# Score steps of the first attention unit between fine steps of a feed-forward block's down sums, and one sequence's sum transfers moved within a round

## The chip, the core and the metric

The kernel runs on one core of a Trainium2 chip. The metric is device time in microseconds of one execution. Five engines work side by side, each through its own instruction queue: PE (TensorE, matmuls; PEld is its weight loads), DVE (VectorE), ACT (ScalarE), POOL (GpSimd), and SP, which here only issues transfers. ACT issues some transfers too. The median before the change is 820.93 us of 3 runs (820.42 to 822.25).

## What is computed

Two sequences of 1024 tokens and 256 channels pass through a "macaron" block: half a feed-forward (FFN), causal attention, half the same FFN.

```
x = x + 0.5 * ffn(layernorm(x))
x = x + attention(layernorm(x))          # 32 heads of 8, 8 key/value heads, rotary, causal
x = x + 0.5 * ffn(layernorm(x))

ffn(x):  h = silu(x @ w_gate) * (x @ w_up)          # 256 -> 1024
         keep of every four neighbours of h the two largest by size
         return h @ w_down                          # 1024 -> 256  ("down sums")
attention: softmax(q k^T / sqrt(8), causal) v, then @ Wo + bo
```

## The kernel before

**Blocks.** The 2048 tokens are four blocks of 512 (`tb` 0 to 3; blocks 0 and 1 are the first sequence). For a block the FFN makes gate and up products (`gate_up`, L238, matmuls at L252), the two-of-four mask in three parts (`mask`, L268: comparisons, ranks, and at L292 the masking of h), and the down sums (`down_half`, L303, matmuls at L307). A block's down sums are two halves of 16 matmuls, each half into one PSUM tile; `down_half` is a generator that yields after every two matmuls. A float32 matmul leaves two records in the trace. `add` (L332, L340 on DVE) adds a finished half to x; `add_aside` (L324) does it with ACT (L329) and POOL (L330).

**Order in the first FFN.** PE and DVE follow an order written out by hand, the string of `first.run` (L941): `g` a step of gate and up, `m` a part of a mask, `d` half of a block's down sums (the generator `down`, L296, runs a half through), `a` an add, `l` layernorm, and `p` a step of the attention's generator: projections of the first sequence, and last the preparation of its first unit. The string ends `g3 p m m m d2 d2 a a`: block 2's down sums on PE beside block 3's last mask on DVE, then two adds.

**Attention.** A unit is one key/value head of one sequence with its four query heads; 16 units, 8 for each sequence. `prepare` (L521) transposes a unit's queries and keys on PE (L529), copies them with ACT (`stage`, L537), and spreads them by 16 transfers into the unit's `qT` and `kT` (L550, L557), and by two more of zeros (L543); for the very first unit SP and ACT share the issuing. `pass1` (L568) makes scores (L584, diagonal masks L599) into one of three PSUM buffers (`ps_big`), and DVE takes negated row maxima from it (L613). `negated` gathers them, POOL splits them (L415, L416), `shift` transposes them (L640) and writes them by four transfers into `qT` (`mrow`, L651). `pass2` makes the scores again, turned and shifted (L669), ACT takes exponentials (L679), and `weighted` sums values (L706). A finished half is copied to `oT` and stored to DRAM (`avs`, L717).

**Rounds.** `round_(n)` (L858) goes through one list, `order` (L770): first-pass steps `p1` (18 in a round) of the current unit, second-pass steps `p2` and `av` of the one before, `prep` of the next. In round 0 there is only a first pass. There PE alternates with `beside_first`, which is `down_slowly(3)` (L318), block 3's down sums through one PSUM tile: two fine steps after each of the first, third, fifth and so on up to the twelfth `p1`, and the rest after the list (L889). Ahead of round 0 POOL clears the buffers of the next two units (`rows`, L397 and L400), in memory that the first FFN gave back. In the rounds PE and POOL keep the order of the text; the other engines and the transfer queues are ordered by a planner, by costs of its own.

**Outputs.** When a sequence's eighth unit has finished a half (`av 2` or `av 9`, L818), `output` (L719) starts: its first step reads the stored sums and heads back by eight transfers on SP (L730, L731); its second takes reciprocals on DVE (L733) and sends them around through DRAM (L735, L737). For the first sequence the first step is taken at once (L825), in rounds 8 and 9, and the second later, after `av 5` of rounds 9 and 10 (L881).

Of the kernel before, what the change touches and what calls it, by code (L numbers as in the profile page):

```python
# [35 lines left out]
def macaron_kernel(  # L36
# [23 lines left out]
    ps_tr = ctx.enter_context(tc.tile_pool(name="ps_tr", bufs=1, space=PSUM))  # L60
    ps_acc = ctx.enter_context(tc.tile_pool(name="ps_acc", bufs=1, space=PSUM))
# [161 lines left out]
    class FFN:  # L223
# [79 lines left out]
        def down_half(self, tb, t2, pool, tag):  # L303
# [11 lines left out]
                        yield  # L315
            self.adds.append((tb, t2, o))

        def down_slowly(self, tb):  # L318

            for t2 in range(2):  # L320
                yield from self.down_half(tb, t2, ps_acc, "acc")
                self.add_aside()
# [26 lines left out]
        def run(self, plan, gens, outs=()):  # L349

            make = {"g": self.gate_up, "d": self.down}
            with tc.manual_schedule(engines={mybir.EngineType.PE, mybir.EngineType.DVE}):
                for op in plan.split():
                    if op == "m":
                        if next(self.masks[0], 0) == 0:
                            self.masks.pop(0)
                    elif op == "a":
                        self.add()  # L360
                    elif op == "o":
                        if next(outs[0], 0) == 0:
                            outs.pop(0)
                            next(outs[0])
                    else:
                        if op not in gens:
                            tb = int(op[1])
                            gens[op] = (
                                make[op[0]](tb)
                                if op[0] in make  # L370
                                else layernorm_T(tb, lambda tb=tb: self.normed(tb), halves=tb == 0)
                            )
                        next(gens[op])

# [9 lines left out]
    def attention(actx, beside_first, beside_last, outs):  # L386
# [413 lines left out]
        def parsed(order):  # L800
            return [(op[0], *map(int, op[1:])) for op in map(str.split, order.split(";"))]

        ops = parsed(order)
        PAIRS = [("av", k) for k in (1, 3, 5, 7)]
        first = max(i for i, op in enumerate(ops) if op[0] == "p1" and op[1] < 3)
        units = [(b, g) for b in range(B) for g in range(NKV)]
        made = {}
        beside = []
        divisions = []

        def step(op, prev, cur, nxt):
            kind, *arg = op
            if kind == "p1" and cur is not None:
                cur.pass1(*steps1[arg[0]], arg[1:] or (0, 1))
            elif kind == "p2" and prev is not None:
                es = prev.pass2(*steps2[arg[0]], arg[1:] or (0, 1))
                made.setdefault(arg[0], (prev, {}))[1].update(es)
            elif kind == "av" and arg[0] in made:  # L818
                unit, es = made.pop(arg[0])
                qh, kbs = steps2[arg[0]]  # L820
                last = arg[0] in (2, 9)
                unit.weighted(qh, kbs, es, last)
                if last and unit.g == NKV - 1:
                    outs.append(output(unit.b, qh))
                    next(outs[-1])  # L825
                    if unit.b < B - 1:
                        divisions.append(outs[-1])
            elif kind == "neg1" and prev is not None:
                prev.negated(1)
            elif kind == "shift":  # L830
                unit = prev if arg[0] == 1 else cur
                if unit is not None:
                    unit.shift(arg[0])
            elif kind == "prep" and nxt is not None:
                nxt.prepare()
# [5 lines left out]
        prev, cur = None, Unit(*units[0])  # L841
        cur.prepare()
        yield
        rctx = ExitStack()
        right = rctx.enter_context(tc.tile_pool(name="att2r", bufs=1, side="right"))
        rows(right)
# [7 lines left out]
        def a_step():  # L854
            while beside and next(beside[0], beside) is beside:
                beside.pop(0)

        def round_(n, prev, cur):  # L858
            nxt = Unit(*units[n + 1]) if n + 1 < len(units) else None
            if n == 1:  # L860
                beside.append(second)
            if nxt is not None and nxt.b == 1:
                for _ in second:
                    pass
            firsts = 0
            for i, op in enumerate(ops):
                step(op, prev, cur, nxt)
                if i == first and cur is not None:
                    cur.negated(0)
                if n == 0 and i == first:  # L870

                    nc.scalar.activation(warm, cur.maxima[0][:, 0, 6:7], AF.Exp, scale=0.0)
                if n == 0 and op[0] == "p1":
                    firsts += 1
                    if firsts <= 12:
                        for _ in range(2 * (firsts % 2)):
                            next(beside_first, None)
                if n > 0:
                    for _ in range(2 if op in PAIRS else op[0] in ("av", "prep")):
                        a_step()  # L880
                if n > NKV and op == ("av", 5) and divisions:  # L881
                    next(divisions.pop(0))
            return cur, nxt

        engines = {mybir.EngineType.PE, mybir.EngineType.Pool}
        with tc.tile_pool(name="att_round0", bufs=2, side="right") as late["2"]:
            with tc.manual_schedule(engines=engines):
                prev, cur = round_(0, prev, cur)
                for _ in beside_first:  # L889
                    pass  # L890
# [6 lines left out]
        with tc.manual_schedule(engines=engines):  # L897
            for n in range(1, len(units)):
                prev, cur = round_(n, prev, cur)
        rctx.close()  # L900
        yield
        with tc.manual_schedule(engines=engines | {mybir.EngineType.DVE}):
            for op in parsed(last_order):
                if op[0] == "b":
                    next(beside_last, None)
                else:
                    step(op, prev, None, None)
            for _ in beside_last:
                pass

    with ExitStack() as fctx:
        actx = ExitStack()
        gens, outs = {}, []

        def second_starts():


            while not second:
                yield
            made = [outs.pop(0), outs.pop(0)]  # L920
            lns = [
                layernorm_T(tb, lambda tb=tb: second[0].normed(tb), copy=nc.vector.tensor_copy)
                for tb in range(2)
            ]

            for k in (0, 1):
                next(made[k])
            yield
            for gen in (made[0], made[0], lns[0], made[1], made[1], lns[0], lns[1], lns[0]):
                next(gen)  # L930
                yield
            for gen in (lns[1], lns[1]):
                next(gen)
                yield

        second = []
        with last_units:
            first = FFN(0, False, f0 := ExitStack(), wd_sb, last_pool)
            att = attention(actx, first.down_slowly(NTB - 1), second_starts(), outs)
            with f0:  # L940
                first.run(  # L941
                    """
                    l0 l0 l0 l1 g0 l1 g0 l2 g0 g0 l2 g0 m l1 g0 g0 l2 m g0 m g1 m g1 m g1 m
                    g1 g1 m g1 d0 m a d0 l3 a p g1 p g1 m g2 m p g2 m g2 m p p p g2 p d1 m m
                    g2 m d1 a a l3 g2 p g2 l3 p g2 m p g3 p p m g3 p p m g3 g3 g3 m g3 m g3
                    m g3 p m m m d2 d2 a a
                    """,
                    {"p": att},
                )
            next(att)  # L950
        next(att)
        early_ctx.close()
        second.append(FFN(1, True, fctx))
        for _ in att:
            pass
        second[0].run(
            """
            o g0 g0 g0 g0 m o g0 g0 o m g0 o g0 m g1 m g1 m g1 m g1 o g1 l2 g1 d0 m l2 g1 g1
            m m m l2 a d0 g2 m g2 o g2 g2 o m a g2 m o l3 g2 l3 g2 d1 m m g2 m m l3 d1 g3 m
            g3 g3 g3 a a g3 m g3 m g3 m g3 d2 m m m a d2 d3 a d3 a a  # L960
            """,
            gens,
            outs,
        )
        actx.close()
# [56 lines left out]
```

## Time and profile before

| | us |
|---|---|
| median of 3 runs (lowest, highest) | 820.93 (820.42, 822.25) |
| the profiled execution's own time | 824.67 |
| its span, first to last instruction | 822.9 |
| third block's down sums on PE | 166.42 to 180.45 |
| first score step of the first unit | 180.37 |
| first second-pass score (round 1 opens) | 210.58 |
| distance of unit preparations (L529) in a round with nothing beside it, as 386.74 to 412.34 | 25.6 |

Times in the profile are microseconds from the span's start. A timeline line has start, length, engine (a q behind it is the engine's queue issuing a transfer), line, operation, tiles written and read, shape, count, and in brackets the engine's idle time before it and what ended it. A line of the view by windows has the window, its length, then busy time and number of instructions of PE, PEld, DVE, ACT and POOL, then the granted share of the TensorE clock, the transfer engines' share, and GB/s. The page's row PEclk gives the granted clock in 40 slices, in tenths.

### The profile page before, as it was taken

How to read it: one execution, taken by the hardware profiler on the slowest of the kernel's cores; microseconds unless marked ns; L12 is line 12 of the kernel's file. 1: busy time of each engine (PE TensorE's matmuls, PEld its weight loads, DVE VectorE, ACT ScalarE, POOL GpSimd, SP SyncE). 2: the span in 40 equal slices, each digit the busy share in tenths (PEclk: the TensorE clock that was granted, in tenths of full speed). 3: DMA queues.
4: the chain of work that ended last, by engine and by line, in shares of the span. 5: the costliest groups of instructions: out<-in, count | busy, mean ns of one | idle time of the engine just before them, and what ended most of it. 6: DMA issues, size and time to landing. Idle time of an engine off the chain costs nothing.

```text
span 822.9 us, 13949 instructions
## 1 busy us (share of the span) xinstructions
PE 786.1 (96%) x5344; PEld 426.4 (52%) x5344; DVE 654.7 (80%) x871; ACT 426.9 (52%) x531; POOL 236.2 (29%) x443
## 2 busy tenths in 40 slices
PE   5999999998899999999999999999999999999998
PEld 2447574476544444454444444444445445657466
DVE  4797999898768796888888788888885479788692
ACT  1331313211677776877787687878877423122210
POOL 3000294821265465464222322233223100000000
PEclk9999999999999999999999899999999999999999
DMA  8100000022213222311333323322202200000001
GB/s 276 31 0 2 0 2 0 0 41 41 33 27 64 44 46 50 67 31 44 66 68 70 93 65 68 56 44 51 57 28 92 74 1 16 1 26 1 11 16 51
DMA packets 31010, 36.03 MB, mean 44 GB/s; under 512 B 12896, under 2 KB 20960, under 8 KB 30944
## 3 DMA queue, kind: packets, MB, share of 16 engines
q1 hardware_dynamic: 29118, 31.85, 17.2%
q10 hardware_dynamic: 1826, 3.29, 1.2%
q8 instruction: 42, 0.69, 0.4%
q14 instruction: 24, 0.20, 0.1%
HBM read 10.75 MB, written 10.75 MB: 26 GB/s over the span
## 4 chain that ended last, share of the span: by engine, by line
PE 71%; DVE 22%; ACT 4%; issue 1%; POOL 1%; DMA 0%; DVEq 0%; ACTq 0%
PE gu L252 20%; PE av L706 16%; PE s L584 9%; PE s L669 9%; PE o L307 9%; DVE maxima L613 8%; ACT e L679 3%; DVE h L292 2%; PE pr L474 2%; PE oo L753 2%; DVE h L262 1%; DVE sg L261 1%; DVE b L275 1%; PE s L599 1%; PE hT L529 1%
## 5 line engine op out<-in xcount | busy, mean ns | idle before, releaser
L613 DVE TENSOR_REDUCE maxima<-s 128x2 f32<-128x1024 f32 (+2 forms) x288 | 343.2, 1220 | 67.2 <-PE s L584 44.3
L679 ACT ACTIVATE e<-s 128x1024 f32<-128x1024 f32 x288 | 287.4, 1023 | 83.4 <-PE s L669 75.1
L706 PE MATMUL av<-e,vaug 128*32 128x512 f32 (+3 forms) x1536 | 158.5, 501 | 0.0
L685 POOL TENSOR_SCALAR_AFFINE_SELECT e<-e 128x256 f32<-128x256 f32 (+1 forms) x224 | 98.3, 451 | 201.5 <-ACT e L679 201.0
L584 PE MATMUL s<-kT,qT 64*128 64x512 f32 (+3 forms) x768 | 133.3, 386 | 14.6 <-ACT e L679 11.7
L669 PE MATMUL s<-qT,kT 64*128 64x512 f32 (+3 forms) x768 | 134.7, 395 | 3.1 <-DVE maxima L613 2.2
L252 PE MATMUL gu<-xnT,wg_sb 128*128 128x512 f32 x256 | 122.3, 600 | 0.7 <-ACT xnT L206 0.7
L252 PE MATMUL gu<-xnT,wu_sb 128*128 128x512 f32 x256 | 120.4, 593 | 0.0
L307 PE MATMUL o<-wd_sb,h 128*128 128x256 f32 x512 | 116.6, 386 | 0.9 <-DVE x L340 0.8
L584 PEld LDWEIGHTS s<-kT,qT 64*128 64x128 f32 x768 | 67.9, 187 | 82.7 <-ACT e L679 37.2
L307 PEld LDWEIGHTS o<-wd_sb,h 128*128 128x128 f32 x512 | 98.1, 193 | 18.5 <-issue 3.7
L669 PEld LDWEIGHTS s<-qT,kT 64*128 64x128 f32 x768 | 67.5, 186 | 62.1 <-DVE maxima L613 32.9
L260 ACT ACTIVATE sg<-gu 128x512 f32<-128x512 f32 x64 | 38.0, 593 | 113.6 <-PE gu L252 113.6
L263 ACT ACTIVATE a<-h 128x512 f32<-128x512 f32 x64 | 40.3, 630 | 104.9 <-DVE h L262 104.8
L252 PEld LDWEIGHTS gu<-xnT,wu_sb 128*128 128x128 f32 x256 | 48.9, 191 | 61.8 <-issue 61.8
L261 DVE TENSOR_TENSOR sg<-sg,gu 128x512 f32<-128x512 f32 x64 | 43.6, 681 | 46.1 <-ACT sg L260 46.0
L252 PEld LDWEIGHTS gu<-xnT,wg_sb 128*128 128x128 f32 x256 | 48.6, 192 | 54.6 <-issue 50.0
L181 POOL TENSOR_TENSOR rstd<-ve,neg_half 128x4 f32<-128x4 f32 x12 | 12.2, 1015 | 194.1 <-DVE ve L179 192.3
L706 PEld LDWEIGHTS av<-e,vaug 128*32 128x32 f32 x1536 | 34.1, 109 | 50.2 <-issue 38.8
L262 DVE TENSOR_TENSOR h<-sg,gu 128x512 f32<-128x512 f32 x64 | 43.9, 687 | 2.2
L599 PE MATMUL s<-half_id,half_mask 64*128 64x64 bf16 (+1 forms) x768 | 43.8, 205 | 0.0
L292 DVE SCALAR_TENSOR_TENSOR h<-w,h 128x512 f32<-128x512 bf16 x64 | 43.7, 743 | 0.0
(80 smaller groups left out, 562.4 us busy)
## 6 DMA issues: line engine op xcount, KB each, us to landing
avs<-oT SPq DMA_DIRECT2D x32, 256.0 KB
qT<-stage SPq DMA_DIRECT2D x124, 64.0 KB
kT<-stage SPq DMA_DIRECT2D x124, 32.0 KB
qT<-mrow SPq DMA_DIRECT2D x128, 4.0 KB
heads<-avs SPq DMA_DIRECT2D x16, 128.0 KB
out<-x SPq DMA_DIRECT2D x7, 256.0 KB
wu_sb<-in_wu SPq DMA_DIRECT2D x2, 512.0 KB
wg_sb<-in_wg ACTq DMA_DIRECT2D x2, 512.0 KB
```

Of the source, the lines that this page charges most:

```text
L252: nc.tensor.matmul(out=gu[:, i, :], lhsT=w_sb[:, kc, gb, j, :], rhs=self.xnT[tb][:, kc, :], start=(kc == 0), stop=(kc == 1),)
L261: nc.vector.tensor_tensor(sg, sg, gu[:, 0, :], ALU.mult)
L262: nc.vector.tensor_tensor(h[:, j, :], sg, gu[:, 1, :], ALU.mult)
L292: nc.vector.scalar_tensor_tensor(h[:, j, :], w[:, j, :], at, h[:, j, :], op, ALU.mult)
L307: nc.tensor.matmul(out=o[:, i, :], lhsT=self.hms[tb][k // 4][:, k % 4, bass.ts(2 * t2 + i, P)], rhs=self.wd_sb[:, k // 4, k % 4, :], start ...
L584: nc.tensor.matmul(out=to[:, i, s, bass.ds(col, n)], lhsT=self.qT[strip, pair, bass.ts(qt, P)].bitcast(FR), rhs=self.kT[strip, bass.ds(kc ...
L599: nc.tensor.matmul(out=last.rearrange("p (t n) -> p t n", n=P)[:, :, bass.ts(h, STRIP)], lhsT=half_mask[strip, h, :], rhs=half_id[strip, N ...
L613: ins = nc.vector.tensor_reduce(dst, src, AX.X, ALU.max, negate=True)
L669: nc.tensor.matmul(out=to[:, i, s, bass.ds(col, n)], lhsT=self.kT[strip, bass.ts(kb, P)].bitcast(FR), rhs=self.qT[strip, pair, bass.ds(q0, ...
L679: nc.scalar.activation(e, to, AF.Exp, scale=SCALE)
L685: nc.gpsimd.affine_select(out=first, in_=first, pattern=[[0, 2], [0, len(pairs)], [1, P]], compare_op=ALU.is_ge, fill=0.0, base=0, channel ...
L706: nc.tensor.matmul(out=self.av[32 * i : 32 * i + 32, TB - n : TB], lhsT=vaugs[self.b][:, kb, bass.ds(self.g * VW, 32)], rhs=es[i][:, bass. ...
```

## The change

Block 2's down sums get a finer generator (`down_finely`, letter `e`), and the first six `p1` steps of the first unit move out of round 0 to stand between them: 11 fine steps and the first add, then score and fine step in turn, six times, then the second add. Round 0 skips those six, and takes one fine step of block 3's sums after each of its 12 remaining score steps, and one more after every fourth. The first step of the first sequence's two outputs, with its eight transfers, is kept back until `av 4` of the same round.

```diff
+        def down_finely(self, tb):
+
+            for t2, (pool, tag) in enumerate(((ps_acc, "acc"), (ps_tr, "tr"))):
+                yield from self.down_half(tb, t2, pool, tag)
...
-            make = {"g": self.gate_up, "d": self.down}
+            make = {"g": self.gate_up, "d": self.down, "e": self.down_finely}
...
-                        next(gens[op])
+                        next(gens[op], None)
...
+        HEAD = 6
...
+        stored = []
...
                     outs.append(output(unit.b, qh))
-                    next(outs[-1])
                     if unit.b < B - 1:
-                        divisions.append(outs[-1])
+                        stored.append(outs[-1])
+                    else:
+                        next(outs[-1])
...
         cur.prepare()
         yield
+        scores = [op for op in ops if op[0] == "p1"]
+        for op in scores[:HEAD]:
+            step(op, prev, cur, None)
+            yield
...
             for i, op in enumerate(ops):
+                if n == 0 and op in scores[:HEAD]:
+                    continue
                 step(op, prev, cur, nxt)
...
                     firsts += 1
-                    if firsts <= 12:
-                        for _ in range(2 * (firsts % 2)):
-                            next(beside_first, None)
+                    for _ in range(1 + (firsts % 4 == 0)):
+                        next(beside_first, None)
...
                 if n > NKV and op == ("av", 5) and divisions:
                     next(divisions.pop(0))
+                if op == ("av", 4):
+                    for out_ in stored:
+                        next(out_)
+                    divisions.extend(stored)
+                    stored.clear()
...
-                    m g3 p m m m d2 d2 a a
+                    m g3 p m m m e2 e2 e2 e2 e2 e2 e2 e2 e2 a e2 e2 p e2 p e2 p e2 p e2 p e2 p e2 a
```

## The prediction, made before the change was run

> **What bounds the kernel now.** The first view is the page. It is a TensorE kernel, and the profiled execution has a few stretches of lowered clock.
>
> ```profile
> span 822.9 us, 13949 instructions
> PE 786.1 (96%) x5344; PEld 426.4 (52%) x5344; DVE 654.7 (80%) x871; ACT 426.9 (52%) x531; POOL 236.2 (29%) x443
> PEclk9999999999999999999999899999999999999999
> ```
>
> A busy PE is not yet a PE doing useful work, so the second view is PE's timeline across the edit, from the third block's down sums (L307, 64 records, two to a matmul) to the first second-pass scores (L669), which open round 1.
>
> ```profile
> 166.42 14.03 PE L307 MATMUL o<-wd_sb,h 128*128 128x256 f32 x64
> 180.37 0.51 PE L584 MATMUL s<-kT,qT 64*128 64x256 f32 x4
> 181.85 1.99 PE L307 MATMUL o<-wd_sb,h 128*128 128x256 f32 x8 [0.84 <-DVE x L340]
> ...
> 189.93 0.50 PE L584 MATMUL s<-kT,qT 64*128 64x512 f32 x2
> 190.26 0.23 PE L599 MATMUL s<-half_id,half_mask 64*128 64x64 bf16 x4
> 190.33 0.48 PE L584 MATMUL s<-kT,qT 64*128 64x512 f32 x2
> 190.65 0.23 PE L599 MATMUL s<-half_id,half_mask 64*128 64x64 bf16 x4
> 190.82 1.99 PE L307 MATMUL o<-wd_sb,h 128*128 128x256 f32 x8
> ...
> 200.40 0.50 PE L584 MATMUL s<-kT,qT 64*128 64x512 f32 x2 [0.78 <-DVE maxima L613]
> ...
> 204.51 6.14 PE L307 MATMUL o<-wd_sb,h 128*128 128x256 f32 x16
> 210.58 0.50 PE L669 MATMUL s<-qT,kT 64*128 64x512 f32 x2
> ```
>
> PE works through the third block's sums without a gap. Then 18 score steps alternate with the fourth block's sums, and from about 199.6 PE only follows DVE's maxima. The last 16 records take 6.14 us where 16 x 0.219 = 3.5 us would do (14.03/64 = 0.219). The third view, DVE's timeline, shows why scores could not simply come earlier: DVE is at the last mask (L292) until 181.2, its first maxima start at 182.32, and later it has nothing for 4.15 us.
>
> ```profile
> 178.71 2.49 DVE L292 SCALAR_TENSOR_TENSOR h<-w,h 128x512 f32<-128x512 bf16 x4
> 181.12 1.28 DVE L340 SCALAR_TENSOR_TENSOR x<-o,x 128x512 f32<-128x512 f32 x2
> 211.49 3.73 DVE L613 TENSOR_REDUCE maxima<-s 128x4 f32<-128x1024 f32 x3 [4.15 <-PE s L599]
> ```
>
> The fourth view, busy time by window, explains the slow tail: the granted clock (the column after POOL) is halved for 6.83 us right after a window in which PE was busy 1.43 of 3.41 us, and once more in round 10.
>
> ```profile
> 199.19:202.60 3.41, 1.43 (x8) 0.37 (x4) 3.41 (x4) 0.00 (x0) 0.00 (x0) 1.00 0.14 24
> 202.60:209.43 6.83, 6.68 (x22) 4.90 (x23) 4.74 (x7) 0.00 (x0) 0.00 (x0) 0.50 0.01 2
> 308.41:311.82 3.41, 3.41 (x24) 1.42 (x26) 2.74 (x3) 2.46 (x3) 3.41 (x4) 0.50 0.52 82
> 465.42:472.25 6.83, 6.83 (x51) 3.21 (x49) 4.24 (x5) 3.59 (x4) 1.73 (x4) 0.50 0.32 48
> ```
>
> The last view is what the first unit's scores need: 16 transfers of K and Q. Their last issue is
>
> ```profile
> 176.61 0.54 ACTq L557 DMA_DIRECT2D qT<-stage  x1
> ```
>
> and its last semaphore count stands in the trace at 179.04.
>
> **The stage, part by part.** Everything up to 166.42 stays. I price PE's pieces from the timeline. A diagonal score step takes 0.40 us before another score (189.93 to 190.33) and 0.49 before a down sum (190.33 to 190.82). In the same way a step off the diagonal costs 0.36, a two-tile step 0.55, a step with eight masks 0.60 to 0.65. Eight down records up to the next score last 1.92 (188.00 to 189.92), that is 1.75 of work and 0.17 of change-over, so a step of two matmuls (four records) costs 0.876 + 0.17 = 1.05. Before a transpose (L529, L640) the change-over is missing. These prices put the work from 180.37 at 23.3 us, an end at 203.7. The trace ends at 210.58, so 6.9 us are lost: 0.84 for the add, 2.6 to the clock, some 3.4 to DVE's maxima. That is all the change can win here.
>
> After the change PE does 11 fine steps (44 records, 9.64 us), and is at the first score at 166.42 + 9.64 = 176.06. In the trace of before this score waits for nothing, because 20 records more stand ahead of it. Now it meets the transfers: 179.04 - 176.06 = 3.0 us of new idle time, and in PE's order the other ten matmuls of the block are queued behind it. The issue times do not move (ACT's copy of the stage at 168.90 comes from L529 at 165.45), so I take 3.0; with the last transfer needed only by the second pair the wait is 2 at least.
>
> From 179.05: six score steps 3.00 (0.65, 0.36, 0.55, 0.49, 0.55, 0.40), five fine steps 5.25, the next unit's transposes (`prep`) 0.86: 188.16. The three score buffers do not hold PE: DVE's maxima start at 181.8 after one add (0.64) instead of two, every 1.14 us, and the fourth score comes at 183.8, after the first maxima's end at 183.0. The second add (0.64) now stands behind the sixth maxima, where DVE has slack.
>
> Then round 0: twelve scores 5.20, 16 fine steps of 0.876 = 14.02, eleven change-overs less the saving before the transposes 1.73, the shift's transposes 0.54: 21.49, so 209.65 without waits. Two waits come in. POOL's memsets of the next two units' buffers wait for the last matmul of the third block (before at 180.56, <-PE o L307); that now ends at 187.0. They and the memset of vaug take 6.0 us (180.56 to 186.56), the split of the maxima 0.53 more, so the shift's transposes can start at 193.65 while PE is there at 192.53: 1.12 us. If the vaug memset slips behind the split it is 0.4; I take 1.12, the order the trace shows. And the fourth block's second half follows its first with one score between, while ACT must copy out the first (0.60): 0.4 us. Round 1 then opens at 211.2, 0.6 later than before. SP's transfers for the next unit move 1 to 2 us later, end near 201 and are needed after 211: nothing. The add and the fine steps as instructions are the same ones as before: nothing.
>
> So the idle time and the clock loss are won back (6.9), and paid for by 3.0 + 1.5 of new waits and some 3 us of change-overs (18 alternations where there were 8).
>
> **The clock.** A 3.0 us gap in a dense stretch is itself a low window. The three drops start 105.8 and 157.0 us apart, 31 and 46 times 3.413, so the windows lie on a fixed grid which the work meets anywhere. The Trainium skill ("TensorE: Matmul & The Clock Gate", section "What's actually happening") says that the half clock comes after at least one *idle* window of about 3.4 us, free-running. By that rule a gap of 3.0 never fills a window and costs nothing: 0.6 us in all. The row disagrees: a window busy 1.43 of 3.41, never idle for long, was followed by the half clock. By the row a window needs about 2 us of idle; a 3.0 us gap gives that in about two grid positions of three. I take the row. The price is one window at half speed in work that PE bounds, 3.41/2 = 1.7 us; two windows, as at 202.60, would be 3.4, but there PE had little to do in the first, so 308.41 is the nearer row. The stage: 0.6 + 1.7 = +2.3 us, none without the drop to +4 with two.
>
> **The transfers in mid-round.** Eight transfers for each of two outputs move behind `av 4`; no instruction is added. In the trace the first lot runs at 434.03 to 437.6, behind a zeros transfer, and the mrow transfers at 437.74 are 0.2 late against a clean round of 25.65 us; the second lot splits the four mrow transfers (the fourth goes at 459.57, some 6 us late), yet the scores that need it start at 461.44, as far behind their neighbour (0.70) as in a clean round. So SP's delay is hidden and its removal wins nothing. What rounds 9 and 10 do lose, 1.30 and 2.86 us beyond 25.65 (438.0, 464.9, 493.45), is two reciprocals of 0.94 us on DVE (443.13, 462.86) and the half clock at 465.42. The reciprocals stay, and the planner places them. I take 0; both hidden would be -1.3, both worse +1.3, and the clock there either way 2.9.
>
> **The sum.** 822.9 + 2.3 = 825.2 us of span for an execution like the profiled one (824.67 with what lies around it). That one stands 3.7 above the median of 820.93, with the same stage in it, so I add the difference to the median: 823.3.
>
> **Rivals.**
> Clock kept: the grid or the rule is kind, and the stage alone counts: +0.6, 821.5, or 820.8 with the memset out of the way. For it: PE is dense on both sides of the gap. Against: the row at 199.19.
> Faster: in rounds 9 and 10 the earlier sums let DVE take both reciprocals in idle time, so PE is not held at the next unit's transposes (0.80 at 464.94), no low window forms and no half clock follows: up to -4.2, with half of it likely to be seen in an average execution, -2.1 to -2.9; with the clock kept at the gap as well, 818.7. It decides from 1.3 us saved there on. Against: the emission of the reciprocals is unmoved.
> Not what it says: SP's order is planned, and the transfers moved in the text may be issued where they were; the stage alone remains, inside the first two cases.
> Much slower: two windows at half clock, or the sums at the head of SP's queue holding zeros and mrow for a round: 825.5 and more.
>
> **Chances.** Half clock at the gap, 823.3 (821.8 to 825): 0.42, of it 0.06 within 0.2%. Clock kept: 0.24, all within. Faster: 0.26. Much slower: 0.08. So faster 0.26, within 0.2% (1.6 us, about what a measurement of this kernel can tell) 0.30, slower 0.44. The range, 818.4 to 825.7, leaves out half of the faster case's far side and most of the last.
>
> **What would show it.** PE idle from 176 to 179 with a transfer or nothing as releaser; a row of half clock soon after 179, none near 203; two-record-pair groups of L307 between scores, L640 waiting for POOL near 193; round 1's first L669 at 211 to 213. Intervals of the unit transposes (L529) in rounds 9 and 10 still above 25.65. I am wrong if the first score runs well before 179, if the change-overs shrink in the fine order, or if round 1 opens before 210.

## The result, and the profile after

The changed kernel takes 828.92 us (827.91 to 829.89, 5 runs) beside 820.93 us (820.42 to 822.87, 5 runs) of the kernel before: 1.0094 times as long, 95% interval 1.0082 to 1.0107. It is slower by 8.0 us; the text on record had 823.3, at most 825.7.

Three lines of the page. No instruction was added: counts are those of before and busy times nearly so. PE's busy time grew by 3 us, and half clock does not account for it: the shown trace of before has more of it (17.1 us) than this one (13.65 us). Part is the finer order itself: e11 below, which has it and no half clock, shows 782.3 us beside 782.0 of a trace of before with 6.83 us of half clock (b0_again).

```profile
span 826.7 us, 13949 instructions
PE 789.2 (95%) x5344; PEld 426.2 (52%) x5344; DVE 656.0 (79%) x871; ACT 426.6 (52%) x531; POOL 236.1 (29%) x443
PEclk9999999989999999999999999999999999999999
```

PE's timeline over the edit, the view that carried the prediction (the lines of before's L584 and L669 are L590 and L675 here, each number 6 higher):

```profile
167.08 9.71 PE L307 MATMUL o<-wd_sb,h 128*128 128x256 f32 x44
177.63 0.35 PE L590 MATMUL s<-kT,qT 64*128 64x256 f32 x1 [0.83 <-DMA kT<-stage]
179.34 0.96 PE L590 MATMUL s<-kT,qT 64*128 64x256 f32 x3 [1.36 <-DMA kT<-stage]
...
180.47 2.08 PE L307 MATMUL o<-wd_sb,h 128*128 128x256 f32 x4
...
188.02 1.13 PE L307 MATMUL o<-wd_sb,h 128*128 128x256 f32 x4
189.08 0.50 PE L590 MATMUL s<-kT,qT 64*128 64x384 f32 x4
...
197.27 0.41 PE L646 MATMUL mT<-ident_r,ms 128*8 128x128 f32 x4 [0.53 <-POOL ms L422]
...
205.34 1.99 PE L307 MATMUL o<-wd_sb,h 128*128 128x256 f32 x8 [0.26 <-ACT half L334]
...
215.09 0.50 PE L675 MATMUL s<-qT,kT 64*128 64x512 f32 x2
```

The first moved score is let in by the transfers, as foretold: the block's 44 records end at 176.8, one matmul gets through at 177.63, the other three at 179.34. Then the same four-record group that takes 1.13 us at 188.02 takes 2.08 at 180.47. The windows say why (the clock stands after POOL's column, busy time of PE second):

```profile
176.54:179.95 3.41, 1.09 (x9) 0.53 (x8) 3.41 (x8) 1.28 (x1) 0.00 (x0) 1.00 0.42 77
179.95:186.78 6.83, 6.83 (x29) 4.18 (x29) 5.28 (x8) 0.00 (x0) 0.00 (x0) 0.50 0.00 0
```

After the gap's window the clock is halved for 6.83 us, in a stretch in which PE is busy throughout: that costs its full half, 3.4 us. The second loss lies 290 us further on. Before, the four head sums of an output (L737 before, L743 now) left SP ahead of the four transfers of a row's maxima, as in a second trace of before (b0_again, below):

```profile
461.21 1.75 SPq L737 DMA_DIRECT2D heads<-recs  x4
463.06 2.48 SPq L651 DMA_DIRECT2D qT<-mrow  x4
```

After, the planner puts them between the third and the fourth. SP's queue, then PE in the same microseconds:

```profile
468.42 1.90 SPq L657 DMA_DIRECT2D qT<-mrow  x3
470.42 2.64 SPq L743 DMA_DIRECT2D heads<-recs  x4
473.10 0.59 SPq L657 DMA_DIRECT2D qT<-mrow  x1
```

```profile
474.82 0.49 PE L675 MATMUL s<-qT,kT 64*128 64x512 f32 x1 [0.93 <-DMA qT<-mrow]
```

The fourth transfer starts 2.7 us late for the four that slipped in, and the score that needs it waits 0.93 us; 3.41 us of half clock follow at 476.91. Another 3.41 us, at 449.61, come some 23 us ahead of the late transfer, so they are not its work.

The best division of the 8.0 us compares this trace with that second one of the kernel before: span ends 826.69 and 818.75, so 7.94 to explain. The third block's sums start 0.85 later (167.08, 166.23). The stage, from there to the first L669 or L675, takes 48.01 instead of 44.25: +3.76. Rounds 9 and 10, between unit transposes, take 27.71 + 28.33 = 56.04 instead of 26.97 + 25.63 = 52.60: +3.44. The rest is equal to 0.1. Of the 3.44, round 10 has 2.70, with the wait and the half clock behind it, and round 9 has 0.74, with the half clock at 449.61.

The later start was made in the kernel's first microseconds, ahead of anything the change touches. There every trace has matmuls of about 1.06 us, where the same ones take 0.59 us later, and how long this lasts differs. The second group of four matmuls, in after and in b0_again:

```profile
14.75 2.56 PE L252 MATMUL gu<-xnT,wu_sb 128*128 128x512 f32 x4
14.83 1.90 PE L252 MATMUL gu<-xnT,wu_sb 128*128 128x512 f32 x4
```

The third group starts at 17.15 against 16.57: 0.58 of the 0.85 stand there already, and the rest has come by 140 us, also ahead of the changed steps.

### The profile page after: what moved, and what is told of

It reads as the page before. It is cut to its first block, busy times and chain, and to the rows that moved or that the text cites. A ratio compares the mean times of both kernels' runs of the same rounds, so it can differ in the third digit from the quotient of the medians.

```text
span 826.7 us, 13949 instructions
## 1 busy us (share of the span) xinstructions
PE 789.2 (95%) x5344; PEld 426.2 (52%) x5344; DVE 656.0 (79%) x871; ACT 426.6 (52%) x531; POOL 236.1 (29%) x443
## 3 DMA queue, kind: packets, MB, share of 16 engines
q1 hardware_dynamic: 29118, 31.85, 17.1%
## 4 chain that ended last, share of the span: by engine, by line
PE 72%; DVE 20%; ACT 4%; DMA 2%; issue 1%; POOL 1%; SPq 0%; DVEq 0%; ACTq 0%; POOLq 0%
PE gu L252 20%; PE av L712 16%; PE s L590 9%; PE s L675 9%; PE o L307 9%; DVE maxima L619 8%; ACT e L685 3%; PE pr L480 2%; DVE h L292 2%; PE oo L759 2%; DVE h L262 1%; DVE sg L261 1%; PE s L605 1%; PE hT L535 1%; DVE b L275 1%
## 5 line engine op out<-in xcount | busy, mean ns | idle before, releaser
L590 PE MATMUL s<-kT,qT 64*128 64x512 f32 (+3 forms) x768 | 135.2, 386 | 14.7 <-ACT e L685 11.7
L675 PE MATMUL s<-qT,kT 64*128 64x512 f32 (+3 forms) x768 | 135.5, 395 | 4.2 <-DVE maxima L619 2.2
L307 PE MATMUL o<-wd_sb,h 128*128 128x256 f32 x512 | 119.0, 388 | 0.3 <-ACT half L334 0.3
L590 PEld LDWEIGHTS s<-kT,qT 64*128 64x128 f32 x768 | 68.5, 187 | 85.6 <-ACT e L685 36.9
L675 PEld LDWEIGHTS s<-qT,kT 64*128 64x128 f32 x768 | 67.5, 185 | 62.9 <-DVE maxima L619 33.6
```

The lines of the kernel that those rows point to most:

```text
L307: nc.tensor.matmul(out=o[:, i, :], lhsT=self.hms[tb][k // 4][:, k % 4, bass.ts(2 * t2 + i, P)], rhs=self.wd_sb[:, k // 4, k % 4, :], start ...
L590: nc.tensor.matmul(out=to[:, i, s, bass.ds(col, n)], lhsT=self.qT[strip, pair, bass.ts(qt, P)].bitcast(FR), rhs=self.kT[strip, bass.ds(kc ...
L675: nc.tensor.matmul(out=to[:, i, s, bass.ds(col, n)], lhsT=self.kT[strip, bass.ts(kb, P)].bitcast(FR), rhs=self.qT[strip, pair, bass.ds(q0, ...
```

## The experiments

Each ratio is against runs of the kernel before on the same chip, whose medians lay between 820.77 and 821.65. Where two experiments are compared, the text takes the difference of their medians; by the ratios it can differ by up to 0.8 us. In the plans below, `e2` is a fine step of block 2 and not a run.

**The kernel before again (b0_again).** No edit.

> The kernel before, unchanged, for a second trace. Its profiled execution stood 3.7 us above its median, so the difference of the two spans (3.8 us) explains only half of the 8.0 us of the medians. If the first trace was an odd one, this trace has a span near 819 and misses one or two of the three clock drops (at 202.6, 308.4 and 465.4 us): which ones it misses tells where a typical execution before saves the 3.7 us. If tracing itself costs 3.7 us, the span is again near 823. Times: 820.9 either way.

820.62 us, ratio 1.0002 (0.9990 to 1.0013). Its trace has one half clock, 6.83 us at 202.60 inside the stage, and neither of the two that the shown trace of before had in rounds 4 and 10 (308.42, 465.43): that trace was of an execution 3.7 us above its median, and the quieter one is the one to compare with.

**One part each (e1_stage, e2_transfers, e3_pacing).** e1 is the change with the output's steps left in `step` as before; e2 is the kernel before with `stored`, filled and emptied as in the change, alone; e3 is the kernel before with only the pace of the down sums in round 0 altered:

```
e3, against before:
-                    if firsts <= 12:
-                        for _ in range(2 * (firsts % 2)):
-                            next(beside_first, None)
+                    for _ in range(1 + (firsts % 4 == 0)):
+                        next(beside_first, None)
```

> The moved score steps and the finer order alone; the sums' transfers stay where they were before. Theory S (stage: the wait of 3 us for the first unit's transfers, and the half clock for two windows that follows it): 827.5 to 829, nearly all of the 8.0 us. Rival T (the moved transfers hold the rows of shifts in SP's queue in round 10, where the trace after shows PE waiting 0.93 us for mrow): 824 to 825, half of it. The trace should again show PE idle for about 3 us before the first score and half clock right after.

> The sums' transfers in mid-round alone; the stage as before. Theory S: 820 to 822, no difference. Rival T: 823.5 to 825.5, with the fourth mrow transfer of round 10 behind the transfers of the reciprocals and PE waiting for it. A gain (under 819.3) would speak for the faster case of the prediction.

> Only the pacing in round 0 is changed: one fine step of the fourth block's sums after every score step, two after every fourth, as in the kernel after; all 18 scores stay in round 0, none is moved ahead, so there is no early wait for transfers. By the prediction's prices 6 to 7 more change-overs cost 1.5 to 2 us of PE, but the low stretch before 202.6 and the half clock after it (2.6 us) should go: 819 to 821. If the change-overs are what makes the kernel after slow: 823 or more.

e1: 825.04 us, 1.0052 (1.0033 to 1.0072). e2: 822.68 us, 1.0018 (1.0008 to 1.0027). e3: 823.31 us, 1.0030 (1.0022 to 1.0039). So the stage alone costs about 4 us and the transfers alone 1.8; together they cost 8.0, more than 5.9. e1 came out at rival T's figure; e2 lies between the two foretold ranges. In e1's trace the half clock after the gap lasts 10.24 us and the stage 49.55, but that execution took 829.33 us, 4.3 above the median, and has a further 6.83 us of half clock in round 10 (469.78), where nothing was moved. In e2's the order of SP's queue is that of after, and PE waits 1.02 us for the same transfer (468.64); rounds 9 and 10 take 53.70 us there, 1.1 more than in b0_again, without half clock. e3 came out at the figure foretold for dear change-overs, but its trace gives another reason. It shows what becomes of the half clock that the stage of before contains: the stage gets shorter, 42.94 against 44.25, but the half clock is not gone. It comes when the stage is over, and lasts twice as long:

```profile
209.01:222.66 13.65, 13.18 (x88) 8.12 (x88) 11.20 (x19) 7.15 (x8) 3.41 (x9) 0.50 0.14 23
```

Between unit transposes, rounds 0 and 1 then last 29.03 and 30.87 us, against 27.98 and 28.84.

**The first scores later or earlier (e4_late, e6_late_stage, e7_early).** The plan of the change with the first score behind 14 fine steps, and behind 8 in place of 11:

```
e4:  e2 x9 a e2 x5 p e2 p e2 p e2 p p p a      (e6: the same, output's steps as in e1)
e7:  e2 x8 p e2 p a e2 p e2 p e2 p e2 p e2 e2 e2 e2 a
```

> The kernel after with the first moved score after 14 fine steps of the third block instead of 11, so that it comes about 178.5 us, when most of its transfers have landed; three scores follow without a fine step between. Theory S: the 3 us wait falls under 1 us, no half clock follows there, and the stage loses 3 to 6 of its excess: 823 to 826. Rival D (the half clock is only displaced, as in the pacing run, where it came back in round 1 for 13.65 us): the wait goes, but a drop of 7 to 14 us appears at 205 to 225, and the time is 826 to 829.

> The late first score of e4 together with the sums' transfers where they were before. By S and Q the two losses add up and both are mended: 819.5 to 822. By D: 823 to 825.

> The other way: the kernel after with the first moved score after 8 fine steps, 1.3 x 2 = 2.6 us earlier, so PE waits some 5.5 us for the same transfers. S: 2.6 us more than after, since PE bounds the stage: 831 to 832.5. If what costs is not the wait but the clock and the change-overs: no more than 829.5.

e4: 825.51 us, 1.0043 (1.0031 to 1.0055). e6: 825.76 us, 1.0040 (1.0024 to 1.0057), a miss: without the wait for transfers it should have come out at or below before. e7: 830.06 us, 1.0095 (1.0077 to 1.0113), between the two foretold ranges, with waits of 3.30 and 1.31 us and 10.24 us of half clock. e4 lies in theory S's range, though not for S's reason, since a half clock came all the same. Later scores do escape the transfers, but then three stand in a row, PE waits for DVE's maxima (window busy 1.78 of 3.41 in e4, 1.82 in e6), and the half clock comes at 187.5 and 186.6, 6.83 us long. The idle time was moved to another releaser, and the half clock went with it. Both traces have half clock in round 10 too (474.26 and 466.49), e6 with its transfers left where they were.

**The output's next step earlier (e5_division).** The change, with one constant altered. The four head sums are emitted when `divisions` is popped, so this alters where the planner may queue them:

```
-                if n > NKV and op == ("av", 5) and divisions:
+                if n > NKV and op == ("av", 2) and divisions:
```

> The kernel after with the second step of the outputs (reciprocals and their transfers) after av 2 instead of av 5, which by the order of SP's queue leaves the four mrow transfers of round 10 together; everything else is left. Theory Q (in the kernel after, four transfers of the reciprocals stand ahead of the fourth mrow transfer, PE waits 0.9 to 1.0 us for it, and half clock may follow): 825.5 to 827.5, 1.5 to 3.5 under the 828.9 of after. Rival C (the loss in rounds 9 and 10 is only the clock's, set by the grid): 828 to 830.

825.54 us, 1.0043 (1.0026 to 1.0060): 3.4 less than the change (4.2 by the ratios), at the lower edge of theory Q. The head sums leave SP at 461.50, well ahead of the four row transfers, which go together again:

```profile
461.50 1.74 SPq L743 DMA_DIRECT2D heads<-recs  x4
468.21 2.56 SPq L657 DMA_DIRECT2D qT<-mrow  x4
```

Rounds 9 and 10 last 26.35 each, 52.70 in all, within 0.1 of b0_again, with no half clock in them. What is left over is the stage: 49.50 us, with 10.24 of half clock in this trace. The mean granted clock of its nine runs goes from 0.994 (826.64 us) to 0.998 (823.73 us), so how long the half clock lasts differs from run to run.

**Keeping PE busy in the gap (e8_fill, e10_b0_fill).** e8 is e5 with four float32 matmuls 128x384, whose product nothing reads, between the third block's sums and the first score. e10 is the kernel before with one such matmul behind each of the last six scores of round 0, where PE follows DVE. Both do extra work.

```
e8:  nc.tensor.matmul(out=fill, lhsT=wqkv_sb..., rhs=wqkv_sb..., start=True, stop=True)   # x4
e10: if n == 0 and op[0] == "p1" and firsts > 12: one of them
```

> Kernel e5 (the mended order of SP's queue) with four extra float32 matmuls of 128x384 ahead of the first moved score, into a score buffer that nobody reads: PE is busy for about 2.6 us of the wait of 3 us, and everything else keeps its order and its waits. If half of the stage's loss is the half clock that the gap brings on (10.24 us of it in e5's trace, 180 to 190), the clock stays up, the stage falls from 49.5 to 44.5 to 45.5 us, and the time is 820.5 to 822.5. If the loss is the wait itself and the change-overs, nothing changes: 825 to 826.

> The kernel before with one extra float32 matmul of 128x384, read by nobody, after each of the last six score steps of round 0, where PE only follows DVE's maxima. If the half clock at 202.6 in the kernel before is brought on by that low stretch, it goes, the last 16 records of the fourth block's sums take 3.5 instead of 6.1 us, and the time is 817.5 to 819.5. If it is only displaced into round 1: 820 to 823.

e8: 822.15 us, 1.0006 (0.9993 to 1.0019), 3.4 less than e5 (3.0 by the ratios). The filling ends just as the transfers are in, and the window stays at full clock:

```profile
175.67 2.74 PE L856 MATMUL fill<-wqkv_sb 128*128 128x384 f32 x8
178.34 0.92 PE L590 MATMUL s<-kT,qT 64*128 64x256 f32 x4
179.33 1.13 PE L307 MATMUL o<-wd_sb,h 128*128 128x256 f32 x4
```

```profile
176.54:179.95 3.41, 3.34 (x21) 2.00 (x20) 3.41 (x9) 1.28 (x1) 0.00 (x0) 1.00 0.26 42
180.00:215.00 35.00, 33.55 (x219) 21.94 (x218) 26.90 (x28) 6.23 (x9) 10.14 (x13) 1.00 0.16 26
```

The stage falls from 49.50 to 44.92 us. PE reaches its first score no sooner than in e5; what is gone is the half clock, and all of its 14 runs have a mean granted clock of at least 0.998. So of the stage's loss some 3 us of the median are the clock. With both mended, the change makes no difference that these runs can tell. e10 kept the clock too, but came to 821.21 us, 0.9994 (0.9982 to 1.0007): the stage takes 43.67, only 0.6 less than in b0_again. Its last 16 records take 3.62 us instead of 6.22, but with the fillers PE reaches them 2.0 us later in the stage; and the stage itself starts 0.6 later. The half clock was not displaced into round 1.

**Bringing the data earlier (e9_prep, e11_prep_pool, e12_pool).** e9 is e5 with the first unit's preparation one gate and up step earlier. In e11, GpSimd issues the half of its transfers that ACT issued. e12 is e5 (preparation unmoved) with SP issuing two and GpSimd three of five.

```
e9:  g3 m p g3 m m m e2 ...        # was  g3 m g3 p m m m e2 ...
e11: e9, queues = itertools.cycle([nc.sync] if self.b or self.g else [nc.sync, nc.gpsimd])
```

> Kernel e5 with the first unit's preparation one gate-and-up step (3.4 us) earlier, so that its 16 transfers land near 175, before the first moved score. If wait and half clock are the stage's whole loss, both go: the stage at 41 to 43 us, the time 817.5 to 820.5, under the kernel before. If the half clock comes back later (in round 1, as with the pacing alone): 821 to 824. If change-overs and POOL's late memsets are the loss: 824 or more.

> The kernel of e9_prep with one thing altered: of the first unit's transfers, the half that ACT issued is issued by GpSimd, which in e9_prep's trace has nothing between its split at 161.68 and its memsets at 192.35. PE's, DVE's and SP's orders are those of e9_prep. In e9_prep ACT's last sigmoid of the gate and up sums stood behind ACT's transfers for 4.67 us, and with it the masks, the adds and the maxima, so that the fourth score waited 4.18 us for a buffer. Theory (ACT held by its own issues is what spoiled the earlier preparation; the stage itself can be won once the first scores have their data): the sigmoid runs at about 169.8, no 4 us wait at the fourth score, no wait for transfers above 1 us at the first, stage 42 to 44.5 against 47.67 in e9_prep and 44.25 before, time 819 to 822; with no half clock anywhere 818.5. Rival 1 (the half clock comes with the stage whatever the order): a drop of 3.4 to 13.7 us between 180 and 220 all the same, stage 45 to 48, time 822.5 to 826. Rival 2 (issues by GpSimd land later than ACT's, whose landing no trace here has measured): PE waits 2 to 5 us for the transfers at about 178.5, half clock after it, time 824 to 829.

> The kernel of e5_division (the stage of the change, transfers mended) with its preparation where it was; only the first unit's transfers are shared out differently: SP issues two of five, GpSimd three of five, ACT none. In e11_prep_pool GpSimd issued one in 0.51 to 0.62 us, SP and ACT in e5_division one in 0.53 to 0.76. The issues then end near 175.2 instead of 177.5, the last one's data should be in near 177, and PE is at the first score at 176.3. Theory (the gap of 2 to 3 us is what brings on the half clock, and without it the stage is worth about as much as in e11_prep_pool, 42.5 us): a wait of 0.5 to 1.2 us, no half clock before 200, stage 43 to 44.5 (49.50 in e5_division, 44.25 before), time 819 to 821.5. Rival (the half clock is due to this place and grid position, not to the gap's length): a drop between 176 and 190 of 6.8 us or more as in e5_division, stage 47 to 49.5, time 823.5 to 826.

e9: 827.72 us, 1.0064 (1.0042 to 1.0087), a miss: 824 or more was foretold for dear change-overs or late memsets, and the cause was another. Earlier issues met a sigmoid that stood behind them on ACT, and PE paid 13 us after that, through DVE. ACT, then PE:

```profile
174.46 0.60 ACT L260 ACTIVATE sg<-gu 128x512 f32<-128x512 f32 x1 [4.67 <-DMA qT<-stage]
```

```profile
187.43 0.64 PE L590 MATMUL s<-kT,qT 64*128 64x512 f32 x2 [4.18 <-DVE maxima L619]
```

e11 frees ACT (the sigmoid runs at 169.05) and reaches 821.35 us, 0.9995 (0.9981 to 1.0009): 6.4 less than e9 (5.7 by the ratios) by who issues eight transfers. It is the only variant of the change that had no wait for transfers, no filler in its place and no half clock in the stage:

```profile
164.67 1.98 PE L252 MATMUL gu<-xnT,wg_sb 128*128 128x512 f32 x4 [1.38 <-DVE h L262]
...
168.21 9.66 PE L307 MATMUL o<-wd_sb,h 128*128 128x256 f32 x44
177.80 0.50 PE L590 MATMUL s<-kT,qT 64*128 64x256 f32 x4
...
210.72 0.50 PE L675 MATMUL s<-qT,kT 64*128 64x512 f32 x2
```

The stage takes 42.51 us, 1.74 less than before: this is what the new order is worth with waits of no more than 0.54 us in its way, against a stage of before that has 6.83 us of half clock. But with the transposes ahead of it, the last gate and up step waits 1.38 us for DVE, and the stage starts 1.98 later (168.21 against 166.23). The two cancel.

e12 is a miss: 824.78 us, 1.0047 (1.0030 to 1.0063). The issues end at 176.6, 1.0 earlier than e5's in a stage that itself started 1.3 later, but the data are in only at 181.1:

```profile
178.65 0.35 PE L590 MATMUL s<-kT,qT 64*128 64x256 f32 x1 [0.96 <-DVE u L282]
181.13 0.74 PE L590 MATMUL s<-kT,qT 64*128 64x256 f32 x3 [2.13 <-DMA qT<-stage]
```

The trace says which queue was late: the nine issues by GpSimd landed a median of 5.0 (kT) and 5.1 us (qT) after they were issued, the last at 181.04. So the gap was not shortened, half clock of 6.83 us came all the same, and the kernel did not make the trial it was meant for: whether a gap of 1 us would have kept the clock is open.

## Why the prediction was wrong

The direction was right (slower had the largest chance, 0.44), the size was not: +2.4 was forecast, +8.0 came. The sum was 0.6 for the stage without new half clock, 1.7 for the clock and 0 for the transfers. The traces of after and b0_again have 0.35, 3.41 and 3.44 in these places, and 0.85 for the later start. So the two terms that failed are the size of the clock term (step 3) and the nought for the transfers (step 4). By its own steps:

1. **"3.0 us of new idle time" at the first score: right in kind, somewhat less in size.** PE is done at 176.8 and can go on at 179.34; one of the four matmuls runs in between, so PE is idle for 2.19 us.
2. **The prices of the steps: right in sum, in part by luck.** A fine step with its change-over was put at 1.05, and 188.02 to 189.08 is 1.06. From the first full-clock score of round 0 (191.92) to round 1 (215.09) the trace has 23.17 us, the sum 21.49 + 1.12 + 0.4 = 23.0, though the split into waits is not the one foretold: POOL's 1.12 was 0.53, since the memset of vaug slipped inside the split, the 0.4 for ACT was 0.26, and scores, sums and change-overs took 0.9 more than priced. The errors cancel. With no wait for transfers and no half clock the sum gives 44.16 + 0.6 - 3.0 = 41.8 us; e11, in just that case, has 42.51.
3. **"One window at half speed, 1.7 us": mis-sized.** Two windows came in the trace of after, three in e1 and e5, with PE busy almost throughout: 3.4 to 5.1 us. (e7 has three as well, but PE waits in the first.) The step chose the row at 308.41 over the row at 202.60, because there PE had little to do; after's two windows came with PE busy for 6.83 of 6.83 us. e8 shows the size: with the clock kept, some 3 us of the median are back. The step also took from one row that "a window needs about 2 us of idle". Its own trace did not bear that out: the window ahead of 308.41 had PE busy 2.73 of 3.41 us, the one ahead of 465.42 2.17. The rule of the Trainium skill ("TensorE: Matmul & The Clock Gate", section "What's actually happening"), half clock after at least one idle window, was rightly set aside: windows with PE busy 0.20 (e9) to 1.82 of 3.41 us (e6) brought it on in this stage.
4. **"I take 0" for the transfers in mid-round: failed.** It was argued that SP's delay was hidden before, so its removal would win nothing, which looked at one sign only. The planner, given a later emission, put the four head sums between the third and fourth row transfer, where they delay a score by 0.93 us. e2 measures this alone at +1.8 us, e5 takes 3.4 us off the change by one constant. That the removal itself wins nothing was right: e5, with the eight transfers moved and the head sums early, is no faster than e1, where they stayed in place (825.54 and 825.04). The bounds of -1.3 and +1.3 were drawn from what those rounds had lost before; a new order of a planned queue can cost more than the old one lost.
5. **"I add the difference to the median": the base was sound, the reading of it was not.** The stage in that trace was like that of b0_again (44.16 and 44.25 us), and the step did no harm there. But rounds 4 and 10 of that execution had half clocks that b0_again lacks, so the faster rival's "up to -4.2" in rounds 9 and 10 had nothing there to win.
6. **"Idle time and clock loss are won back": the idle time yes, the clock no.** In e3, e4 and e6 it moved with the work to the next thin window. Only where the gap was filled or gone (e8, e11) was there no half clock in the stage.

The rivals: the much slower one (two windows, or the sums in SP's queue; 825.5 and more, chance 0.08) is what happened, and both of its halves did, though the head sums held up one transfer of a row and not a whole round. They were joined by "or", though nothing kept them apart.

Two things stay open. The start of the third block's sums is decided in the first microseconds, as shown above: the longer the slow matmuls there, the later it is (third group at 16.13 in e2 and the sums at 166.09; 16.57 and 166.23 in b0_again; 17.15 and 167.08 in after; 18.02 and 167.97 in e12). Why this differs, and whether it recurs in every run of a kernel, was not seen. And the transfers cost 1.8 us alone but 3.4 to 3.9 with the stage. The wait for the late transfer is in every trace with the split order (0.93 in after, 1.02 in e2, 1.05 in e4, 1.25 in e7). The half clock in rounds 9 and 10 is not tied to it: traces with the transfers left in place lose 2.9 us there (before, e1, e6) or nothing (b0_again, e3, e10), and e4, with them moved, is no slower than e6 without (825.51 and 825.76). All five runs of the change have a mean granted clock of 0.990 or 0.991, which is what its trace has, so its half clock seems to recur; which part of it the late transfer brings on is not shown.

## What to carry to other kernels

Before you move the first use of some data forward, take the time at which its last transfer lands from the trace, and price the gap not by its own length but by what the clock does after it: here a wait of 2.6 us (176.8 to 179.34) was followed by half clock that cost another 3.4 (5.1 in e5's trace), and matmuls that nobody reads, put into the gap, took some 3 back. When a DMA's emission moves under a planner, write out the new order of its queue and ask what now stands behind it; a constant (`av 5` to `av 2`) was worth 3.4 us. And when transfers are issued by a computing engine, look at which compute stands behind them on it: eight issues on ACT, moved some 3 us forward, cost about 6 us beside the same issues on GpSimd (e9, e11).

## What the runs showed of the hardware that was not expected

- The drops of the clock start at whole multiples of 3.413 us from each other within a trace (after: 179.95, 449.61 and 476.91 are 79 and 8 such spans apart), so one can lay windows of that length over the whole trace. In the fifteen traces, the first 20 and the last 10 us left out, every such window at full clock with PE busy 1.84 us or less was followed by half clock (1.84 in e4, 470.85), and none with 2.8 or more. In between it went either way: 1.99 and 2.44 (after) and 2.73 (before, 305.00) were followed by it, 2.02 (e9, 163.74) and 2.45 (e2, 468.17) were not. A few matmul records are missing from such traces, so a single busy time can be somewhat low.
- The half clock lasts for 1 to 4 spans of 3.41 us, and neither how thin the window before it was nor dense work during it settles how many: busy 1.09 was followed by two spans (after), 1.16 by three (e5), 0.66 by two (e12), 0.20 by one (e9, at 187.63), 1.56 by four (e3).
- The transfers that GpSimd and SP share in e12 were in 4.5 us after the last issue's end (176.6 to 181.1); in e5, shared by SP and ACT, within 1.4 (177.5 to 178.9). GpSimd issued one in 0.51 to 0.62 us, SP and ACT one in 0.53 to 0.76. GpSimd's landed a median of 5.0 to 5.5 us after their issue (e11, e12). In e11 this did no harm, as the last of them was in at 176.3 and PE came for it at 177.80.
